# A two-layer vision tower: in its last stage small softmax steps go to GpSimd, the head products are cut into half tiles, and the hand-written order is replaced

## The chip, the cores and the metric

The kernel runs on one core of one Trainium2 chip. Its engines work side by side, each through its own queue in program order: TensorE multiplies matrices (PE in the profile; its weight loads are PEld), VectorE (DVE) and ScalarE (ACT) work element by element, GpSimd (POOL) does the same and also starts some transfers, and SyncE (SP) starts the other transfers (DMA). An instruction that needs another engine's result waits for a semaphore, and all that stands behind it in its queue waits with it. The metric is device time in microseconds (us) for one execution. Three executions of the kernel before took 1803.8, 1806.92 and 1807.66 us; the median is 1806.92 us.

## The reference, cut to what matters

32 images of 256x256 pixels become 256 tokens of 256 numbers each. Layer 0 (attention and a feed-forward part) and the attention of layer 1 come first and are not touched. The change lies in the feed-forward part of layer 1, which has four heads of 64 numbers and, inside every head, four experts:

```python
sx = jnp.einsum('bsh,ndh->bnsd', x, hl_w) + hl_b[None, :, None, :]       # head products
q = jnp.einsum('bnsd,neod->bneso', sx, wq)                               # one query per expert
k = jnp.einsum('bnsd,nod->bnso', sx, wk); v = jnp.einsum('bnsd,nod->bnso', sx, wv)
scores = jnp.einsum('bnesd,bntd->bnest', q, k) * d ** 0.5 + causal
att = jax.nn.softmax(scores, axis=-1)
qkv = jnp.einsum('bnest,bntd->bnesd', att, v)
gs = jax.nn.softmax(gate logits of the four experts, axis=-1)            # first gate
mixed = jnp.einsum('bnsed,bnse->bnsd', out, gs)
hn = layernorm(mixed + resid, ln_g, ln_b)                                # a norm over 64
hx = relu(fx @ fc1_w.T + fc1_b); hx = hx @ fc2_w.T + fc2_b               # zero masks left out here
fout = layernorm(hx + fx, fnorm_g, fnorm_b)
fg = jax.nn.softmax(fout @ fgate_w.T, axis=-1)                           # second gate
return fout * fg                                                         # per head; h is added to it
```

All of it is in 32-bit floats.

## The kernel before, in words

The kernel keeps all 32 images (`H[b]`, 128 tokens by 2 by 256) on the chip and goes through five stages. The last one, called the E stage here, starts at about 1240 us and takes 570 us of the 1812 us. Each image goes through the same 96 or so *pieces*, short functions that issue a few instructions each, listed in `PIECES`. What matters here, in the order in which one image needs it:

- `features_in` (SP loads the image's features), `heads` (PE: four 128x128 products over 256 columns; each 32-bit product shows as two matmul records), `heads_out` (ACT copies them out, SP makes a copy with the halves exchanged), `residual` (for the first four images alone).
- `experts`, `head_values`, `scores` 0 to 4, `exponentials` 0 to 4 (ACT), `outputs` 0 to 3 (PE), `outputs_out` 0 to 7 (ACT). The products of scores, experts and head values are cut into 64x64 tiles, those of `outputs` into 64x64 tiles at first and then 128x64 tiles.
- `gate_logits` and `gate_softmax` 0 to 6: the first gate, on tiles of 128 tokens by 8 (token half and head) by 4 experts. Step 0 takes the maximum, 1 subtracts, 2 is ACT's exponential, 3 the sum, 4 the reciprocal, 5 and 6 multiply. All but step 2 are on VectorE.
- `mixed` 0 and 1 (two VectorE products of 128x1024), `summed` 0 to 2, `squares`, `squares_sum`, `root`, `scaled`: the weighted sum of the experts and its norm.
- `turn_e` (VectorE transposes in blocks, SP writes to memory), `moved_e` (SP reads it back), `turned_e` (ACT), `features_moved` (SP), `first_layer` (PE), `first_layer_out` (ACT, then four SP transfers), `second_layer` (PE, 128x64 tiles), `second_layer_out` (VectorE).
- `head_gate` 0 to 8: the second gate, on tiles of 128 by 2 by 4, and for step 0 and 1 by 4 more. Step 0 multiplies, 1 sums, 2 adds a row, 3 maximum, 4 subtracts, 5 is ACT's exponential, 6 sums, 7 reciprocal, 8 multiplies.
- `last_norm` 0 to 5: three VectorE steps of 128x512, eight of 128x64 that multiply with the gate and add `h`, and the transfer to the output.

No scheduler orders this: `tc.manual_schedule` puts the instructions on each engine in exactly the order in which the pieces are called. The order is a list written out by hand. `ROUND` is one turn of a software pipeline: an entry (-7, 3) means that in round r piece 3 is issued for image r+7. Before the change `heads` is at -7 and the last pieces are at -1, so an image is in work for seven rounds. When `heads` of the last image (31) has been issued, `order_e` leaves the round and issues `END`, a list of all that is left, where an entry (2, 40) means piece 40 of image 31-2. The rounds run for 1240 to 1735 us and `END` from there.

Results of PE go to eight banks that are handed out in turn by `bank()`; a round takes 29 of them, so PE waits if a bank's last contents have not been read. Several tiles have one or two buffers (`fxT`, `both`, `fout`: one; `sx`, `g`, `exT`, `eo`, `ey`: two). For the last image `turn_e` and what follows avoid the way through memory.

The lines that the text names, by their numbers in the kernel before: 118 all products, 1173 and 1179 `heads_out`, 1206 `experts_out`, 1250 `exponentials`, 1285 `outputs_out`, 1349 and 1354 `gate_logits`, 1362 to 1376 `gate_softmax`, 1380 `mixed`, 1388 to 1394 `summed`, 1428 and 1433 `turn_e`, 1440 `moved_e`, 1449 `turned_e`, 1487 and 1490 `first_layer_out`, 1502 `second_layer_out`, 1510 to 1532 `head_gate`, 1537 to 1549 `last_norm`. Lines 151, 152, 842, 856 and 857 are from the stage before (the attention of layer 1), where GpSimd is in use.

Of the kernel before, what the change touches and what calls it, by code (L numbers as in the profile page):

```python
# [33 lines left out]
F32 = mybir.dt.float32  # L34
AF = mybir.ActivationFunctionType
ALU = mybir.AluOpType
AX = mybir.AxisListType
# [3 lines left out]
P = 128  # L41
B, N, D = 32, 256, 256
NC = N // P
HALF = B // 2
KSEL = 127
NH, NE, HD = 4, 4, 64
# [34 lines left out]
def vit_tower(tc, a, out):  # L81

    nc = tc.nc
# [33 lines left out]
    def mm(o, lhsT, rhs, first=True, last=True):  # L117
        nc.tensor.matmul(o, lhsT, rhs, start=first, stop=last)  # L118

    def over(ap, shape, axis):  # L120
        return ap.unsqueeze(axis).to_broadcast(shape)
# [184 lines left out]
    with (  # L306
# [7 lines left out]
        for k, n in enumerate(PARTS):  # L314
            f = sum(PARTS[:k])
            x, w = pw.tile([P, n, N], F32, name=f"patch0_{k}"), pw.tile([P, n, D], F32, name=f"tokW{k}")
# [797 lines left out]
    with (  # L1114
# [49 lines left out]
        def heads(b, im):  # L1164
            p = im.ph = bank()
            for hp in range(2):
                for k in range(2):
                    mm(p[:, hp * N : (hp + 1) * N], hl[:, k, hp * P : (hp + 1) * P], im.f[:, k], k == 0, k == 1)

        def heads_out(b, im):  # L1170
            im.sx = p2.tile([P, 2, N], F32, name="sx")
# [166 lines left out]
        def gate_logits(b, im, i):  # L1338
# [14 lines left out]
            if i == 2:  # L1353
                nc.vector.tensor_reduce(
                    gate_in[b % 2][:, :, 1:], im.lg.rearrange("p g e x -> p g x e"), AX.X, ALU.add
                )

        def gate_softmax(b, im, i):
            x = gate_in[b % 2]
            if i == 0:  # L1360
                im.m = small("sm_m", [P, NG])
                nc.vector.tensor_reduce(im.m, x, AX.X, ALU.max)
            if i == 1:
                im.gate = small("gate", [P, NG, NE])
                nc.vector.tensor_tensor(im.gate, x, over(im.m, [P, NG, NE], 2), ALU.subtract)
            if i == 2:
                nc.scalar.activation(im.gate, im.gate, AF.Exp)
            if i == 3:
                im.m = small("sm_m", [P, NG])
                nc.vector.tensor_reduce(im.m, im.gate, AX.X, ALU.add)  # L1370
            if i == 4:
                nc.vector.reciprocal(im.m, im.m)
            if i == 5:
                nc.vector.tensor_tensor(im.gate, im.gate, im.rden, ALU.mult)
            if i == 6:
                nc.vector.tensor_tensor(im.gate, im.gate, over(im.m, [P, NG, NE], 2), ALU.mult)

        def mixed(b, im, k):
            x = experts_of(im, k, MIX, HD)
# [127 lines left out]
        def head_gate(b, im, i):  # L1507
            if i == 0:
                im.lg = small("lg2", [P, NC, NH, NH])
                nc.vector.tensor_tensor(  # L1510
                    im.lg.rearrange("p c n x -> p (c n) x"), im.whole["ey"][:, :, HD:],
                    over(im.rs, [P, NG, NH], 2), ALU.mult,
                )
            if i == 1:
                im.gate = small("fgate", [P, NC, NH])
                nc.vector.tensor_reduce(im.gate, im.lg.rearrange("p c n x -> p c x n"), AX.X, ALU.add)
            if i == 2:
                nc.vector.tensor_tensor(im.gate, im.gate, over(fg_row, [P, NC, NH], 1), ALU.add)
            if i == 3:
                im.m = small("sm_f", [P, NC])  # L1520
                nc.vector.tensor_reduce(im.m, im.gate, AX.X, ALU.max)
            if i == 4:
                nc.vector.tensor_tensor(im.gate, im.gate, over(im.m, [P, NC, NH], 2), ALU.subtract)
            if i == 5:
                nc.scalar.activation(im.gate, im.gate, AF.Exp)
            if i == 6:
                im.m = small("sm_f", [P, NC])
                nc.vector.tensor_reduce(im.m, im.gate, AX.X, ALU.add)
            if i == 7:
                nc.vector.reciprocal(im.m, im.m)  # L1530
            if i == 8:
                nc.vector.tensor_tensor(im.gate, im.gate, over(im.m, [P, NC, NH], 2), ALU.mult)

        def last_norm(b, im, i):
            f = whole(im, "eblk" if b == B - 1 else "fout", G8)
# [37 lines left out]
            (features_moved,), (count_bad, 0), (count_bad, 1), (count_bad, 2), (count_bad, 3),  # L1573
        )
        ROUND = (
            (-2, 2), (-3, 54), (-1, 72), (-3, 56), (-4, 42), (-6, 4), (-1, 73), (-4, 33), (-1, 74), (-4, 34),
            (-4, 44), (-3, 57), (-4, 45), (-1, 75), (-3, 58), (-3, 59), (-6, 1), (-6, 5), (-4, 43), (-1, 76),
            (-4, 46), (-6, 6), (-5, 16), (-5, 12), (-5, 22), (-1, 77), (-6, 30), (-5, 18), (-2, 67), (-6, 9),
            (-1, 87), (-5, 13), (-4, 47), (-5, 14), (-2, 92), (-2, 69), (-6, 10), (-1, 78), (-5, 19),
            (-6, 11), (-1, 79), (-3, 60), (-4, 48), (-5, 20), (-3, 61), (-6, 7), (-5, 15), (-2, 68),  # L1580
            (-1, 80), (-2, 70), (-1, 89), (-3, 62), (-1, 81), (-4, 49), (-1, 82), (-6, 8), (-1, 88),
            (-3, 63), (-3, 64), (-1, 83), (-5, 31), (-1, 84), (-4, 50), (-5, 32), (-1, 85), (-1, 86),
            (-7, 3), (-8, 0), (-1, 90), (-3, 65), (-5, 21), (-4, 51), (-1, 91), (-5, 41), (-3, 66), (-5, 40),
            (-5, 39), (-4, 52), (-4, 53), (-4, 55), (-2, 71), (-1, 93), (-1, 94), (-1, 95), (-1, 96),
        )
        END = (
            (0, 2), (3, 51), (4, 65), (2, 40), (3, 52), (2, 39), (2, 42), (2, 41), (2, 21), (0, 1), (3, 53),
            (4, 66), (3, 54), (3, 55), (5, 71), (3, 56), (6, 90), (3, 57), (5, 72), (4, 2), (2, 33), (2, 34),
            (0, 4), (5, 73), (5, 74), (3, 58), (2, 43), (5, 75), (2, 44), (3, 59), (1, 15), (5, 76), (2, 46),
            (2, 45), (5, 77), (2, 47), (5, 78), (6, 91), (2, 48), (0, 7), (1, 21), (4, 67), (3, 60), (0, 9),  # L1590
            (2, 49), (3, 61), (4, 92), (2, 50), (5, 79), (4, 69), (0, 10), (0, 5), (0, 8), (2, 51), (3, 62),
            (2, 52), (5, 80), (0, 11), (5, 87), (2, 53), (3, 63), (1, 13), (4, 70), (3, 64), (2, 54),
            (5, 81), (2, 55), (4, 68), (1, 14), (5, 82), (2, 56), (3, 65), (0, 6), (5, 89), (3, 66), (2, 57),
            (1, 19), (1, 16), (1, 12), (1, 20), (0, 12), (5, 83), (5, 88), (4, 71), (1, 18), (1, 22),
            (2, 58), (0, 18), (4, 72), (3, 2), (4, 73), (2, 59), (4, 74), (4, 75), (1, 31), (1, 32), (1, 33),
            (1, 41), (1, 34), (1, 42), (1, 39), (1, 40), (4, 76), (3, 67), (2, 60), (5, 84), (0, 30),
            (5, 85), (3, 69), (2, 61), (5, 86), (5, 90), (1, 44), (3, 68), (0, 13), (1, 43), (2, 62),
            (1, 45), (2, 63), (3, 92), (1, 46), (5, 91), (3, 70), (0, 14), (1, 47), (4, 77), (0, 16),
            (2, 64), (1, 48), (4, 78), (1, 49), (4, 79), (1, 50), (4, 80), (1, 51), (2, 65), (1, 52),
            (1, 53), (4, 81), (2, 66), (0, 22), (0, 15), (4, 82), (0, 19), (1, 55), (1, 54), (0, 20),  # L1600
            (4, 87), (3, 71), (4, 83), (1, 56), (0, 31), (4, 89), (1, 57), (4, 84), (3, 72), (0, 21),
            (1, 58), (0, 32), (0, 40), (3, 73), (4, 85), (1, 59), (4, 88), (1, 60), (0, 41), (0, 42),
            (3, 74), (2, 2), (3, 75), (0, 39), (2, 67), (1, 61), (0, 33), (0, 43), (4, 86), (4, 90), (0, 34),
            (0, 44), (3, 76), (3, 77), (1, 62), (1, 63), (2, 69), (2, 92), (3, 78), (4, 91), (2, 68),
            (2, 70), (1, 64), (1, 65), (3, 79), (0, 46), (0, 45), (0, 47), (3, 80), (1, 66), (0, 48),
            (3, 81), (0, 49), (3, 87), (3, 82), (1, 2), (2, 71), (0, 50), (3, 83), (0, 51), (3, 89), (0, 52),
            (3, 84), (3, 88), (0, 53), (3, 85), (0, 55), (0, 54), (2, 72), (2, 73), (0, 56), (2, 74),
            (3, 86), (0, 57), (2, 75), (3, 90), (2, 76), (0, 58), (3, 91), (1, 67), (2, 77), (0, 59),
            (2, 78), (0, 60), (2, 87), (2, 79), (1, 92), (0, 61), (2, 80), (2, 89), (1, 69), (2, 81),
            (1, 70), (0, 62), (1, 68), (2, 82), (1, 71), (2, 83), (0, 63), (0, 64), (2, 84), (2, 88),  # L1610
            (2, 85), (0, 65), (0, 66), (2, 90), (1, 73), (0, 67), (1, 72), (2, 86), (0, 69), (0, 92),
            (1, 74), (1, 75), (2, 91), (0, 70), (0, 68), (0, 71), (0, 93), (0, 72), (0, 73), (0, 74),
            (0, 94), (1, 76), (0, 75), (1, 77), (0, 76), (0, 95), (1, 78), (0, 77), (0, 87), (0, 78),
            (1, 79), (1, 87), (1, 80), (0, 79), (0, 96), (1, 81), (0, 80), (1, 82), (1, 89), (1, 83),
            (0, 81), (0, 89), (0, 82), (0, 83), (1, 84), (1, 88), (0, 84), (1, 85), (0, 88), (0, 85),
            (1, 86), (1, 90), (1, 91), (0, 90), (0, 86), (0, 91),
        )
        LAST = PIECES.index((heads,))

# [407 lines left out]
```

## Time and profile before

| what | us |
|---|---|
| median of three runs | 1806.92 |
| the profiled execution's own time | 1813.98 |
| its span, from the first to the last instruction | 1812.2 |
| PE, DVE, ACT, POOL busy in the span | 1763.8, 1309.8, 776.5, 445.5 |
| first `heads` product of the E stage | 1241.0 |
| steady rounds, 1300 to 1700 us: 24 images | 400 |
| PE busy in them | 395.68 |
| DVE busy in them | 378.09 |
| ACT busy in them | 336.08 |
| POOL busy in them | 0.00 |
| `heads` of the last image | 1735 |
| 1735 to 1812.2: DVE busy, PE busy | 69.93, 44.95 |

The profiled execution took 0.4% longer than the median. A busy PE does not mean that PE is at its peak, since matmuls overlap and their ends are modelled; what the rows of PE give best is when each group of products starts. The same holds for VectorE in small: an instruction's duration has a tail that the next one overlaps, so that a row of instructions takes less than the sum of their durations. The chain that ended last is an account of what released what; a wait that is no part of it cost nothing.

### The profile page before, as it was taken

Reading aid. Unit: us, or ns where it says so; the run is one execution under the profiler, and the core shown is the slowest. Engines: PE = TensorE matmul, PEld = TensorE weight load, DVE = VectorE, ACT = ScalarE, POOL = GpSimd, SP = SyncE. Lnnn points to the kernel's source line nnn. Section 1 sums busy time; section 2 is a strip of 40 time slices with the busy share of each in tenths; the row PEclk is TensorE's granted clock in tenths of the full one; section 3 lists DMA queues with packets and bytes.
Section 4 is the critical chain, followed back from the end, with each engine's and each line's share of the span. In section 5 each row is a group of like instructions: output and inputs, shape, how many; then the busy total and the mean of one; then the engine's idle time right before and its main releaser. Section 6 shows DMA issues by size and latency. Waiting matters only on the chain.

```text
span 1812.2 us, 43832 instructions
## 1 busy us (share of the span) xinstructions
PE 1763.8 (97%) x18072; PEld 1267.4 (70%) x18072; DVE 1309.8 (72%) x3580; ACT 776.5 (43%) x1607; POOL 445.5 (25%) x506
## 2 busy tenths in 40 slices
PE   9999999999999999999999999999999999999993
PEld 7888566667576676767654555557888888888882
DVE  2335367787878665444458877875699999999998
ACT  0000322222222212121244554555888888888883
POOL 1223234343434335333344433341000000000000
PEclk9999999999999999999999999999999999999995
DMA  8552112121211115233312222112244444444432
GB/s 274 180 154 65 35 30 67 51 72 38 59 47 49 57 50 182 91 119 99 112 57 82 75 88 78 74 71 83 68 114 112 115 111 120 109 118 114 122 99 69
DMA packets 197999, 167.93 MB, mean 93 GB/s; under 512 B 71713, under 2 KB 174881, under 8 KB 197409
## 3 DMA queue, kind: packets, MB, share of 16 engines
q1 hardware_dynamic: 191072, 147.49, 28.4%
q0 software_dynamic: 6144, 16.79, 3.1%
q8 instruction: 144, 2.36, 0.6%
q10 hardware_dynamic: 576, 0.79, 0.2%
q14 instruction: 63, 0.51, 0.1%
HBM read 82.95 MB, written 57.41 MB: 77 GB/s over the span
## 4 chain that ended last, share of the span: by engine, by line
PE 85%; DVE 6%; DMA 4%; ACT 4%; issue 1%; SPq 0%; ACTq 0%; DVEq 0%
PE bank L118 85%; DMA er_turned<-eblk 1%; ACT et L1250 1%; DMA fraw<-er_turned 1%; DMA both<-hx 1%; DVE fout L1545 1%; ACT fxT L1449 0%; DMA patch<-in_patches_dram 0%; PE bank L518 0%; DVE eo L1380 0%; ACT g L1206 0%; DVE eblk L1428 0%; DVE ranges L1403 0%; DVE six L126 0%; ACT eo L1285 0%
## 5 line engine op out<-in xcount | busy, mean ns | idle before, releaser
L118 PE MATMUL bank<-ev,et 64*64 64x72 f32 (+3 forms) x6144 | 186.8, 226 | 0.2
L118 PEld LDWEIGHTS bank<-ev,et 64*64 64x64 f32 (+1 forms) x6144 | 171.6, 135 | 10.9 <-ACT hx L1487 1.2
L118 PE MATMUL bank<-tokW,patch 128*128 128x256 f32 x768 | 170.1, 385 | 2.9 <-DMA patch<-in_patches_dram 2.9
L118 PE MATMUL bank<-g,sw 64*64 64x128 f32 (+2 forms) x1280 | 168.0, 377 | 0.0
L1250 ACT ACTIVATE et<-bank 128x512 f32<-128x512 f32 x320 | 167.4, 624 | 1.2 <-PE bank L118 1.2
L118 PE MATMUL bank<-g,sx 64*64 64x128 f32 (+2 forms) x1280 | 167.6, 377 | 0.0
L118 PEld LDWEIGHTS bank<-tokW,patch 128*128 128x128 f32 x768 | 148.5, 194 | 24.9 <-issue 3.8
L118 PE MATMUL bank<-bxT,w_wuv 128*128 128x512 f32 x300 | 131.4, 592 | 0.0
L869 ACT ACTIVATE hT<-bank,cols 128x512 f32<-128x512 f32 x64 | 43.7, 687 | 187.2 <-PE bank L118 122.3
L118 PE MATMUL bank<-wvo,dm 128*128 128x512 f32 x256 | 114.3, 599 | 0.0
L118 PE MATMUL bank<-w_wo,gT 128*128 128x256 f32 x512 | 113.2, 379 | 0.0
L118 PE MATMUL bank<-attn,bv 128*128 128x256 f32 x512 | 113.1, 379 | 0.0
L118 PE MATMUL bank<-w_w,hT 128*128 128x256 f32 x512 | 112.3, 379 | 0.0
L118 PE MATMUL bank<-xsel,w_w 128*128 128x512 f32 x256 | 111.4, 592 | 0.0
L118 PEld LDWEIGHTS bank<-attn,bv 128*128 128x128 f32 x512 | 97.2, 190 | 19.6 <-issue 7.2
L126 DVE BATCH_NORM_STATS2 six<-h 128x6 f32<-128x256 f32 x256 | 105.7, 413 | 4.4
L118 PEld LDWEIGHTS bank<-w_w,hT 128*128 128x128 f32 x512 | 97.0, 190 | 15.6 <-issue 2.9
L118 PEld LDWEIGHTS bank<-w_wo,gT 128*128 128x128 f32 x512 | 97.2, 190 | 13.4 <-DVE gT L491 0.2
L118 PE MATMUL bank<-w_wuv,bxT 128*128 128x512 f32 x240 | 105.4, 592 | 0.0
L1285 ACT COPY eo<-bank 128x280 f32<-128x280 f32 x256 | 89.3, 396 | 36.4 <-PE bank L118 36.4
L118 PEld LDWEIGHTS bank<-bxT,w_wuv 128*128 128x128 f32 x300 | 57.0, 190 | 64.9 <-issue 64.1
L118 PEld LDWEIGHTS bank<-g,sx 64*64 64x64 f32 x1280 | 92.6, 133 | 10.1
(288 smaller groups left out, 3572.3 us busy)
## 6 DMA issues: line engine op xcount, KB each, us to landing
patch<-in_patches_dram SPq DMA_DIRECT2D x31, 768.0 KB
exT<-normed SPq DMA_DIRECT2D x32, 256.0 KB
sw<-sx SPq DMA_DIRECT2D x64, 128.0 KB
er_turned<-eblk SPq DMA_DIRECT2D x31, 256.0 KB
fraw<-er_turned SPq DMA_DIRECT2D x62, 128.0 KB
both<-fxT SPq DMA_DIRECT2D x62, 128.0 KB
both<-hx SPq DMA_DIRECT2D x124, 64.0 KB
out_dram<-fout SPq DMA_DIRECT2D x31, 256.0 KB
```

The costliest lines, as they stand in the source:

```text
L118: nc.tensor.matmul(o, lhsT, rhs, start=first, stop=last)
L126: nc.vector.bn_stats(six, x)
L869: nc.scalar.activation(s.hT[:, m, :], p, AF.Gelu_apprx_tanh, bias=col("b1", m))
L1250: nc.scalar.activation(t2[:, r, :], p, AF.Exp)
L1285: nc.scalar.copy(im.o[:, g * OC : (g + 1) * OC], p[:, 0:OC])
L1545: nc.vector.scalar_tensor_tensor(f[:, g, :], f[:, g, :], im.gate[:, i - 3, n : n + 1], H[b][:, i - 3, d], ALU.mult, ALU.add)
```

## The change

Three edits, all in the E stage.

1. Eight steps of the two gates move from VectorE to GpSimd for all images but the last: `gate_softmax` 3, 5, 6 and `head_gate` 0, 1, 2, 6, 8. The three that are sums become two GpSimd additions each (`added`: four numbers to two, two to one). So GpSimd gets eleven instructions per image.
2. `heads` computes each 128x128 product as two products of 128x64.
3. `ROUND` and `END` are new lists. In the new round `heads` is at -8 and the last pieces are at -1, so an image is in work for eight rounds. On PE the new round is: `head_values`, `scores` 1, `experts` 1, `first_layer`, `scores` 3, `outputs` 0, `heads`, `outputs` 1, `outputs` 2, `second_layer`, `outputs` 3, `scores` 4, `experts` 0, `scores` 2, `scores` 0. Before it was: `outputs` 2, `outputs` 3, `experts` 0, `scores` 4, `scores` 0, `head_values`, `scores` 1, `scores` 2, `first_layer`, `experts` 1, `scores` 3, `outputs` 0, `outputs` 1, `heads`, `second_layer`.

```diff
@@ heads
                 for k in range(2):
-                    mm(p[:, hp * N : (hp + 1) * N], hl[:, k, hp * P : (hp + 1) * P], im.f[:, k], k == 0, k == 1)
+                    for q in halves:
+                        w = hl[:, k, hp * P + q.start : hp * P + q.stop]
+                        mm(p[q, hp * N : (hp + 1) * N], w, im.f[:, k], k == 0, k == 1)
@@ new, ahead of gate_softmax
+        def on_pool(b):
+            return nc.vector if b == B - 1 else nc.gpsimd
+
+        def added(b, o, x, name):
+            shape = [P, o.shape[1], 2] + list(x.shape[3:])
+            if b == B - 1:
+                nc.vector.tensor_reduce(o, x.rearrange("p c n x -> p c x n") if x.ndim > 3 else x, AX.X, ALU.add)
+                return
+            t = p1.tile(shape, F32, name=name)
+            nc.gpsimd.tensor_tensor(t, x[:, :, 0:2], x[:, :, 2:4], ALU.add)
+            nc.gpsimd.tensor_tensor(o, t[:, :, 0], t[:, :, 1], ALU.add)
@@ gate_softmax
             if i == 3:
                 im.m = small("sm_m", [P, NG])
-                nc.vector.tensor_reduce(im.m, im.gate, AX.X, ALU.add)
+                added(b, im.m, im.gate, "sm_4")
...
-                nc.vector.tensor_tensor(im.gate, im.gate, im.rden, ALU.mult)
+                on_pool(b).tensor_tensor(im.gate, im.gate, im.rden, ALU.mult)
             if i == 6:
-                nc.vector.tensor_tensor(im.gate, im.gate, over(im.m, [P, NG, NE], 2), ALU.mult)
+                on_pool(b).tensor_tensor(im.gate, im.gate, over(im.m, [P, NG, NE], 2), ALU.mult)
@@ head_gate (steps 0, 1, 2, 6 and 8 in the same way)
-                nc.vector.tensor_tensor(im.gate, im.gate, over(fg_row, [P, NC, NH], 1), ALU.add)
+                on_pool(b).tensor_tensor(im.gate, im.gate, over(fg_row, [P, NC, NH], 1), ALU.add)
...
@@ ROUND: all 85 entries replaced (the new ones)
+            (-2, 68), (-5, 47), (-2, 75), (-6, 18), (-7, 9), (-5, 48), (-4, 59), (-1, 78), (-3, 67),
+            (-6, 13), (-5, 49), (-4, 60), (-7, 10), (-6, 19), (-1, 79), (-7, 7), (-3, 92), (-3, 69),
+            (-7, 11), (-7, 8), (-4, 61), (-6, 15), (-5, 50), (-4, 62), (-1, 80), (-1, 87), (-6, 31),
+            (-1, 81), (-1, 89), (-4, 63), (-1, 82), (-3, 70), (-5, 51), (-1, 83), (-4, 64), (-1, 88),
+            (-6, 21), (-8, 3), (-6, 32), (-5, 52), (-6, 39), (-6, 33), (-6, 40), (-4, 65), (-1, 84),
+            (-4, 66), (-6, 41), (-9, 0), (-3, 71), (-6, 42), (-5, 53), (-1, 85), (-1, 90), (-5, 55),
+            (-5, 54), (-1, 86), (-5, 56), (-1, 91), (-6, 34), (-5, 57), (-8, 4), (-6, 43), (-7, 16),
+            (-2, 76), (-4, 2), (-6, 44), (-8, 30), (-3, 72), (-3, 73), (-6, 45), (-6, 46), (-5, 58),
+            (-3, 74), (-8, 1), (-8, 5), (-7, 14), (-7, 22), (-8, 6), (-7, 20), (-2, 77), (-7, 12), (-1, 93),
+            (-1, 94), (-1, 95), (-1, 96),
@@ END: 305 entries before, 324 now
...
```

## The prediction

> **What bounds the kernel now.** I read the page first (busy shares over 40 slices), then the E stage in windows, then PE's and VectorE's waits there, then single groups.
>
> ```profile
> PE   9999999999999999999999999999999999999993
> DVE  2335367787878665444458877875699999999998
> POOL 1223234343434335333344433341000000000000
> ...
> 1500.00:1550.00 50.00, 49.97 (x1280) 42.97 (x1271) 47.66 (x145) 42.92 (x109) 0.00 (x0) 1.00 0.45 117
> sum 400.00, PE 395.68 PEld 337.41 DVE 378.09 ACT 336.08 POOL 0.00; mean PE 49.46 PEld 42.18 DVE 47.26 ACT 42.01 POOL 0.00
> ...
> 1740.00:1790.00 50.00, 34.45 (x832) 28.02 (x823) 49.00 (x154) 31.82 (x83) 0.00 (x0) 0.84 0.39 102
> 1735.00:1812.20 77.20, 44.95 (x1007) 35.08 (x1005) 69.93 (x229) 39.45 (x102) 0.00 (x0) 0.75 0.31 85
> ```
>
> The window columns are length, then busy us (and instructions) of PE, weight loads, DVE, ACT, POOL, then clock, DMA share, GB/s. Steady rounds (the sum over 1300 to 1700, 24 images) take 16.67 us each; PE works 16.49 of them, VectorE 15.75, GpSimd nothing. So PE sets the round and VectorE is 0.9 us behind it. In `END` it is turned round: from 1740 to 1790 VectorE is busy 49 of 50 us and PE 34.
>
> ```profile
> DVE ey L1502 <- PE bank L118: 8.2, 23, 1.0
> DVE ranges L1403 <- ACT esq L1399: 5.6, 7, 1.3
> PEld bank L118 <- ACT fxT L1449: 5.2, 6, 1.3
> PE bank L118 <- ACT fxT L1449: 3.8, 5, 1.0
> ...
> 1402.38 0.23 PE L118 MATMUL bank<-ev,et 128*64 128x72 f32 x1
> 1402.53 1.99 PE L118 MATMUL bank<-exT,w_hl_t 128*128 128x256 f32 x8
> 1404.46 1.17 PE L118 MATMUL bank<-W,both 128*64 128x68 f32 x32
> 1405.56 2.81 PE L118 MATMUL bank<-ev,et 64*64 64x72 f32 x96
> ...
> L118 PE MATMUL bank<-exT,w_hl_t x256: 379/379/483, 1241.0 to 1735.2; 128*128 128x256 f32 x128
> ```
>
> The waits (us in all, times, longest, over the 24 rounds) say that VectorE waits for PE, and PE only for `fxT`, the features that come back through memory. The three timeline groups around `heads` are 128x64, 128x128, 128x64.
>
> **Head products in half tiles.** Removed: 8 records of 128x128 per image. Added: 16 of 128x64. The `W,both` group has the added form: 32 records of 68 columns start within 1.10 us, that is in pairs 0.059 us apart, and 68 columns of the 256 that take 0.216 us are 0.057. So two halves run at once, and 16 half records take 8 x 0.216 = 1.73 us, as the 8 whole ones do. What goes is the change of shape on both sides. In the starts of single records: the first head product starts 0.094 us late, the second 0.320 after it instead of 0.216 (the 483 ns beside 379 in the last line), the first `W,both` 0.093 late, its second pair 0.050 late: 0.34 us per image. In the new round `heads` stands between `outputs` 0, which ends in 128x64, and `outputs` 1, which is 128x64, and `second_layer` between `outputs` 2 and 3, 128x64 too; the four changes between 64x64 and 128x64 per round stay. PE is the bound, so 32 x 0.34 = **-10.9 us**. Bounds: 0 (the cost moves to another boundary) and -10.9; I take -10.9, since no 128x128 product is left in the round.
>
> **The order of the round.** PE's stall chain is `turn_e`, transfer, `moved_e`, transfer, `turned_e`, `first_layer`:
>
> ```profile
> 1420.12 0.65 DVE eblk L1428
> 1420.79 5.02 DMA er_turned<-eblk
> 1426.50 3.62 DMA fraw<-er_turned
> 1430.22 0.82 ACT fxT L1449
> 1431.09 2.64 PE bank L118 x44
> ```
>
> That is 10.97 us. Adding the pieces' rows in the lists' order gives the room for it: before, `turn_e` stands at 15.7 us of VectorE's round (stretched to 16.67) and `first_layer` at 8.5 of PE's next, 9.5 us; now at 8.5 and 2.5 of rounds of 16.2, 10.2 us, and VectorE can be up to 1.5 us ahead of PE, as `second_layer_out` comes later in its list. On SP `moved_e` now stands behind the output transfer and `sw` (issued by about 11 of the round, the first transfer lands at 13 to 14), so neither holds it. PE's idle time in the 24 rounds is 4.3 us; I take half of it away, 0.09 x 29 = **-2.6 us**. Bounds: -5.2, and +9 if `second_layer` (its four transfers are issued 2.4 us long and `first_layer_out` stands behind a VectorE-fed step on ACT) or `fxT` costs 0.3 per round.
>
> **The gates on GpSimd.** Removed from VectorE per image: 145 (L1370), 192, 182, 184, 200, 157, 151 and 167 ns, 1.38 us by duration; by starts less, for four 128x64 `fout` steps of 279 ns take 0.78 us in the chain, 0.70 of their sum. I take 1.0: VectorE falls from 15.75 to 14.75. Added to GpSimd: eleven instructions on 2 to 32 numbers per partition. Nearest rows:
>
> ```profile
> L151 POOL TENSOR_SCALAR rs_d<-st_d 128x4 f32<-128x4 f32 x16 | 3.1, 195 | 113.7 <-DVE st_d L127 112.9 <-issue 0.4
> L152 POOL TENSOR_TENSOR rs_d<-rs_d,minus_half 128x4 f32<-128x4 f32 x16 | 16.6, 1036 | 1.3
> L856 POOL TENSOR_TENSOR h<-h,dx 128x512 f32<-128x512 f32 x28 | 36.3, 1297 | 0.0
> ...
> 1196.61 0.77 DVE L842 TENSOR_SCALAR dx<-h,rs_d,d_one 128x256 f32<-128x256 f32 x2
> 1197.68 2.78 DVE L842 TENSOR_SCALAR dx<-h,rs_d,d_one 128x256 f32<-128x256 f32 x2
> ```
>
> L152 is a power, the additions and products are like L856: (1.297 - 0.195) / 508 = 2.2 ns per number on 0.2 us, so 0.2 to 0.26 each, 2.5 us per image (bounds 2.1 and 11): GpSimd is idle enough even at 11.
>
> What it costs VectorE is the open term. The last two lines are the same instruction twice: 0.77 us beside the 1.0 us power of 1196.70, 2.78 beside the additions L856 and L857, which it had to sit out. So a GpSimd instruction on 512 numbers stops VectorE for its whole length, one on 4 numbers not at all. VectorE works 62% of its E time on instructions with two inputs in SBUF. Bounds: 0, and 2.5 x 0.62 = 1.5 us per image. I take 0.5, near the row with few numbers. The Trainium skill ("SBUF — State Buffer", section "Who interferes with whom") speaks against the change: a VectorE instruction with two SBUF inputs and a GpSimd one that reads SBUF take a shared port as an exclusive lock, and the later one is blocked for the whole instruction. The L856 line agrees, the power beside 0.77 us does not; by the rule alone the term would be the 1.5, by the row 0.
>
> New waits: on GpSimd `head_gate` 8 stands behind `gate_softmax` 3, which waits for ACT's `gate_softmax` 2, behind `exponentials` 3 and `root`, which waits for VectorE's `squares_sum` (done at 7.1 of its round). 7.1 + 0.45 + 0.95 + 0.35 + 0.45 + 0.2 + 0.2 = 9.7; `last_norm` 3, whose turn on VectorE is at 9.2, waits 0.5 us. All behind it on VectorE (`mixed`, `second_layer_out`) moves too. VectorE: 14.75 + 0.5 + 0.5 = 15.75, under the new 16.24 of PE. In the rounds the GpSimd edit is worth nothing.
>
> **`END`.** PE's rows over its entries give 34.7 us before, 35.7 now, so it starts 1.0 us sooner (**-1.0**). VectorE's rows (0.60 per 128x512 step, 1.13 per `mixed`, and so on) give 69.7 before (69.93 busy in the window) and, with the moved steps taken out, 70.9: one more round is in flight. **+1.2**. It has 55 GpSimd instructions: at 0.05 us of blocking each **+2.7** (bounds 0 and 7.5), and for answers that come later than VectorE's own **+1.5** (0 to 5). Nothing covers these: VectorE has 1 us idle in 50.
>
> Sum: -10.9 - 2.6 - 1.0 + 1.2 + 2.7 + 1.5 = **-9.1 us**. The profiled execution took 1813.98 us, 0.4% over the median; it would take 1804.9, and the median 1806.92 would be 1798.
>
> **Rivals.**
> - *VectorE becomes the bound* (slower). Place: two-input steps behind GpSimd's. Price at full blocking: 14.75 + 1.5 + 0.7 = 16.95 us per round, +0.28 x 26 = +7, and +10 in `END`: 1824; at half of it about 1811. For: L856, 62%. Against: the 0.77 line. It decides when blocking and new waits pass 1.5 us per image, 16.24 - 14.75; by then `END` has eaten the rest.
> - *`END` gives it back.* The rounds gain 13.5, but blocking and late answers in `END` cost 11 and not 4: 1805, inside 0.2%, which is 3.6 us and about what a measurement can tell from no change. For: VectorE 49 of 50 busy.
> - *The halves don't run at once*: 16 x 0.216, +1.7 us per image, +55: 1858. Against: `W,both`.
> - *More than forecast*: no blocking (-4), all stalls gone (-3): 1791.
>
> **How the numbers follow.** Forecast (1794 to 1803) 0.47, more than forecast 0.14, `END` gives it back 0.14, VectorE bound 0.23, halves one by one 0.02. Faster 0.61, same 0.14, slower 0.25. The likeliest gives 1798, alone 1791 to 1803. For 8 in 10 I go from 1788 (no blocking and a better-packed `END`) to 1816 (half the VectorE rival and more).
>
> **What would show it.** Head records 128*64 without a long first one, 1.73 us from group to group; rounds of 16.2 to 16.3 us with PE 99% busy; fewer waits for `fxT`; GpSimd at 2.5 us per image; `fout` or `eo` steps mostly at 279 and 1216 ns; from `heads` of image 31 to the end 79 to 82 us. Wrong it would be if two-input VectorE steps grow by GpSimd's whole durations, if VectorE waits for POOL over 1 us per image, or if PE waits for `both` or `fxT` in each round.

## The result, and the profile after

The changed kernel took 1803.68 us (median of 15 runs, 1801.22 to 1807.4), beside 1806.92 us (1803.8 to 1809.64) for the kernel before. The ratio is 0.9984, with a 95% interval of 0.9977 to 0.9991: 3 us less where 9 us were forecast, and inside the 0.2% that the forecast counted as "same". The time lies in the stated range of 1788 to 1816 us and the direction is right, but the gain is a third of what was forecast.

The profiled executions make it look larger: 1801.22 us after, 1813.98 us before. That is the fastest of 15 executions beside one slower than all 15 of before. So both kernels were profiled once more in the experiments (1806.12 and 1803.71 us), and differences below are taken between profiles that lie near their medians.

The first view is the same as before: the busy shares in 40 slices of the kernel after.

```profile
PE   9999999999999999999999999999999999999992
...
DVE  3335376887878565443448878875689998999998
...
POOL 1223133443424335242334433331012221222221
```

GpSimd now has work to the end, and VectorE's slices in the rounds are no fuller than before. Next the windows (length, then busy us and instructions of PE, weight loads, DVE, ACT, POOL, then clock, DMA share, GB/s), first in the rounds from 1300 to 1700 us, then in `END`, which runs from 1717.1 us:

```profile
1500.00:1550.00 50.00, 49.82 (x1331) 41.01 (x1326) 45.29 (x120) 43.14 (x110) 10.09 (x33) 1.00 0.41 114
...
sum 400.00, PE 398.37 PEld 331.83 DVE 359.87 ACT 342.37 POOL 78.93; mean PE 49.80 PEld 41.48 DVE 44.98 ACT 42.80 POOL 9.87
...
1720.00:1770.00 50.00, 36.23 (x929) 29.13 (x928) 49.43 (x131) 32.81 (x85) 11.18 (x35) 0.87 0.38 108
1717.10:1799.40 82.30, 45.00 (x1060) 35.42 (x1054) 74.76 (x221) 42.24 (x111) 17.21 (x55) 0.79 0.30 86
```

PE is busy for 99.6% of the rounds, so PE sets them, as forecast. `END` is VectorE's, as before, and takes 82.3 us. The waits of the rounds, the three groups of products around `heads`, and `heads` by its records:

```profile
DVE ranges L1417 <- ACT esq L1413: 19.7, 22, 2.2
...
DVE fout L1559 <- POOL fgate L1546: 8.7, 23, 0.4
...
PEld bank L118 <- ACT g L1208: 5.0, 24, 0.3
...
1408.22 2.22 PE L118 MATMUL bank<-ev,et 64*64 64x72 f32 x64
1410.27 1.90 PE L118 MATMUL bank<-exT,w_hl_t 128*64 128x256 f32 x16
1412.00 2.91 PE L118 MATMUL bank<-ev,et 128*64 128x72 f32 x96
...
L118 PE MATMUL bank<-exT,w_hl_t x512: 379/379/430, 1236.3 to 1718.6; 128*64 128x256 f32 x171
```

`heads` takes 1.73 us from start to start (1410.27 to 1412.00), as forecast, against 1.92 before. PE's waits for `fxT` are down to 0.2 us. In their place stands a wait that was not there: for `g`, the copy of `experts_out`, once in each round, by 0.2 us on the mean.

The forecast said that PE waited only for `fxT` before the change. The same view of the kernel before has one more line, a wait of PE's weight loads in 22 of the 24 rounds, between `heads` and `second_layer`:

```profile
PEld bank L118 <- ACT eo L1285: 7.3, 22, 0.3
```

It goes with the whole head products. With half products in the old order the line is gone; with whole products in the new order the weight loads are idle for 0.33 us behind `heads` again, and there the profile names no other engine as the cause.

The table is the working view of all that follows. It comes from when the first `heads` record of each image starts: the first one, the five intervals in which the pipeline fills, the 26 rounds after them, the round that no wait disturbs (the lowest value that recurs), and the time from the last image's `heads` to the end. "Over" is what the 26 rounds took beyond 26 undisturbed ones. Us, from one profile each; the ratio is of the times, to before.

| kernel | ratio (95%) | first | fill | 26 rounds | undisturbed | over | `END` |
|---|---|---|---|---|---|---|---|
| before, first profile | 1 | 1241.0 | 62.2 | 430.5 | 16.26 | 7.6 | 78.6 |
| before, again | 1 | 1235.8 | 62.2 | 428.1 | 16.26 | 5.2 | 78.3 |
| after, first profile | 0.9984 (0.9977 to 0.9991) | 1236.3 | 60.9 | 419.9 | 16.10 | 1.2 | 82.3 |
| after, again | | 1237.4 | 61.0 | 420.9 | 16.11 | 2.1 | 82.7 |
| before + half tiles | 1.0000 (0.9991 to 1.0009) | 1237.4 | 61.8 | 430.3 | 15.91 | 16.6 | 79.5 |
| before + GpSimd | 0.9996 (0.9988 to 1.0005) | 1236.9 | 62.2 | 427.3 | 16.25 | 4.8 | 79.4 |
| before + both of these | 0.9992 (0.9981 to 1.0003) | 1238.9 | 61.5 | 426.8 | 15.90 | 13.4 | 77.7 |
| new order alone | 1.0070 (1.0057 to 1.0083) | 1235.6 | 62.1 | 429.3 | 16.46 | 1.5 | 87.8 |
| new order + GpSimd | 1.0031 (1.0019 to 1.0044) | 1235.9 | 62.1 | 430.1 | 16.46 | 2.2 | 82.4 |
| new order + half tiles | 1.0006 (0.9997 to 1.0015) | 1235.7 | 61.0 | 421.4 | 16.11 | 2.6 | 89.1 |

From "before, again" to the two profiles of after: the rounds give 7.2 to 8.2 us, the fill 1.2 to 1.3, and `END` takes 4.0 to 4.4 back. The first profile of before had 5.2 us more ahead of the E stage, in code that the change does not touch, and 2.4 us more of stalls.

### The profile page after: what moved, and what is told of

Read it like the earlier page. It is cut to its first block, busy times and chain, and to the rows that moved or that the text cites. A ratio compares the mean times of both kernels' runs of the same rounds, so it can differ in the third digit from the quotient of the medians.

```text
span 1799.4 us, 44514 instructions
## 1 busy us (share of the span) xinstructions
PE 1751.3 (97%) x18328; PEld 1245.9 (69%) x18328; DVE 1273.6 (71%) x3332; ACT 774.3 (43%) x1607; POOL 547.8 (30%) x847
## 4 chain that ended last, share of the span: by engine, by line
PE 87%; ACT 5%; DVE 5%; issue 1%; DMA 1%; SPq 0%; ACTq 0%; POOL 0%; DVEq 0%
PE bank L118 87%; ACT et L1252 2%; ACT g L1208 1%; ACT fxT L1463 1%; DVE fout L1559 1%; PE bank L518 0%; DVE eo L1394 0%; DVE ranges L1417 0%; DMA patch<-in_patches_dram 0%; DVE six L126 0%; ACT dex L950 0%; DVE fout L1553 0%; DMA both<-hx 0%; DVE dz L996 0%; DVE two L1402 0%
## 5 line engine op out<-in xcount | busy, mean ns | idle before, releaser
L118 PE MATMUL bank<-ev,et 64*64 64x72 f32 (+3 forms) x6144 | 197.5, 226 | 2.6 <-ACT et L1252 0.7
L118 PEld LDWEIGHTS bank<-ev,et 64*64 64x64 f32 (+1 forms) x6144 | 179.7, 135 | 19.2 <-ACT g L1208 5.7
L118 PE MATMUL bank<-g,sw 64*64 64x128 f32 (+2 forms) x1280 | 176.4, 380 | 0.0
L118 PE MATMUL bank<-g,sx 64*64 64x128 f32 (+2 forms) x1280 | 175.4, 379 | 0.0
L1252 ACT ACTIVATE et<-bank 128x512 f32<-128x512 f32 x320 | 172.6, 627 | 4.1 <-PE bank L118 2.6
L118 PEld LDWEIGHTS bank<-w_wo,gT 128*128 128x128 f32 x512 | 97.2, 190 | 13.4 <-DVE gT L491 0.2
```

The source lines that it names most:

```text
L1252: nc.scalar.activation(t2[:, r, :], p, AF.Exp)
```

## The experiments

The theory at the start: half tiles give 0.35 us per round, but in the new order a wait of PE for ACT's copies takes half of it; the rival: the 0.35 us is not to be had, or is lost somewhere else.

### Half tiles alone, in the kernel before

```diff
-                    mm(p[:, hp * N : (hp + 1) * N], hl[:, k, hp * P : (hp + 1) * P], im.f[:, k], k == 0, k == 1)
+                    for q in halves:
+                        w = hl[:, k, hp * P + q.start : hp * P + q.stop]
+                        mm(p[q, hp * N : (hp + 1) * N], w, im.f[:, k], k == 0, k == 1)
```

> The kernel before, with the head products in half tiles and nothing else. Theory A (the half tiles are worth what the starts of single records say, 0.34 us per image, and PE is the bound): the group `heads` takes 1.73 us from start to start and the group after it 0.95 (before 1.92 and 1.10), undisturbed rounds 15.92 us instead of 16.26, the time falls by about 10.5 us (0.58%), to 1796 to 1797. Theory B (in after, a wait of PE for ACT's second copy of `experts_out` 1 eats half of it, and that wait comes from the steps being closer together, not from the new order): here too about 0.16 us per round is left, the time falls by about 5 us, to 1802. Rival C (another wait takes the whole place): within 2 us of before.

Measured: 1806.54 us beside 1806.5, ratio 1.0000. It is rival C: another wait takes the whole place. The undisturbed round is 15.91 us, within 0.01 us of what the forecast's terms give (16.26 - 0.34), yet only seven of the 26 rounds are undisturbed. The waits from 1300 to 1700 us:

```profile
ACT fxT L1451 <- DMA fraw<-er_turned: 12.0, 10, 2.1
PEld bank L118 <- ACT fxT L1451: 10.9, 10, 2.0
...
PE bank L118 <- ACT fxT L1451: 8.8, 9, 1.8
...
PEld bank L118 <- DMA both<-hx: 2.3, 5, 0.5
```

PE waited 5.2 us for `fxT` (its weight loads' line) in the kernel before, 3.2 in its second profile, now 10.9. The features' way through memory does not get shorter when PE's round does.

### Whole head products, in the kernel after

The edit is the one above, undone.

> The changed kernel, with the head products in whole tiles again. Theory A (the 0.28 us wait of PE for `experts_out` 1 in each round is a fixed cost of the new order): rounds grow by the whole 0.34 us, to 16.44 us, and the time by 10 to 11 us over after, to about 1814. Theory B (the wait is ACT not getting its copies out in time, and takes up whatever PE gains ahead of it): rounds grow by 0.1 to 0.2 us only, the wait shrinks to under 0.1 us, and the time grows by 2 to 5 us, to 1806 to 1809.

Measured: 1812.35 us, ratio to before 1.0031, 8.5 us (0.47%) more than after. The undisturbed round is 16.46 us, 0.35 more than after's. Theory A: in the new order the half tiles are worth what was forecast, 26 x 0.35 = 9.1 us in the rounds and 1.1 in the fill, and the wait for `g` is a cost of the order that does not shrink when PE has more time ahead of it (that wait's line still has 4.2 us). The group that waits is the 64x64 part of `outputs` 0: 1.03 us from start to start with whole and with half products in the new order, 0.85 in the old one; the other groups, some longer and some shorter by a change of shape, sum to the same. So the new order makes the round 0.19 us longer by itself (0.19 with half products, 0.20 with whole ones).

### One copy of `experts_out` on VectorE

```diff
             for h, p in enumerate(im.pg[hp]):
-                nc.scalar.copy(im.g[:, 2 * hp + h, :, :].rearrange("p j n -> p (j n)"), p)
+                o = im.g[:, 2 * hp + h, :, :].rearrange("p j n -> p (j n)")
+                if hp == 1 and h == 1 and 0 < b < B - 3:
+                    nc.vector.tensor_copy(o, p)
+                else:
+                    nc.scalar.copy(o, p)
```

> The changed kernel, with one of the two copies of `experts_out` 1 (the one that ends the chain of ACT copies for which PE waits in `outputs` 0) on VectorE instead of ACT, in the rounds. If that chain of copies is what keeps the rounds of after at 16.10 instead of 15.85: PE's wait of 0.28 us there goes, rounds of 15.85 to 15.95 us, 4 to 6.5 us less than after, 1797 to 1800. Rival (VectorE, 14.5 us busy per round, slips by the 0.7 us copy and its waits, so that answers come later): rounds stay at 16.1 or grow, 1803 to 1810.

Measured: 1796.8 us (1796.31 to 1800.31), ratio to before 0.9951 (0.9937 to 0.9965), 9 us less than before and 6 less than after (0.33%). ACT's queue ahead of `outputs` 0, first in after, then with the copy moved:

```profile
1405.75 0.87 ACT L1463 ACTIVATE fxT<-fraw,cols 128x512 f32<-128x512 f32 x1
1406.46 1.14 ACT L1252 ACTIVATE et<-bank 128x512 f32<-128x512 f32 x2
1407.41 1.16 ACT L1208 COPY g<-bank 128x512 f32<-128x512 f32 x2
```

```profile
1402.87 1.14 ACT L1256 ACTIVATE et<-bank 128x512 f32<-128x512 f32 x2
1403.83 0.66 ACT L1212 COPY g<-bank 128x512 f32<-128x512 f32 x1
...
1403.54 0.69 DVE L1210 COPY g<-bank 128x512 f32<-128x512 f32 x1 [0.42 <-PE bank L118]
...
1404.63 1.83 PE L118 MATMUL bank<-ev,et 64*64 64x72 f32 x63
```

In after, `outputs` 0 starts at 1408.22 us and needs four banks. `experts` 1, `first_layer` and `scores` 3, which stand just ahead of it, hold two each, so that two of the eight are left; its other two are those of `experts` 1, which ACT has read only at 1408.57, behind `fxT` and two exponentials. PE starts six of the group's records by 1408.34 and the next at 1408.62; `outputs` 0 does not read `g`, so it is the bank that it waits for:

```profile
1408.62 0.89 PEld L118 LDWEIGHTS bank<-ev,et 64*64 64x64 f32 x32 [0.21 <-ACT g L1208]
```

With one copy on VectorE both are read before PE comes (the later one ends at about 1404.5, PE starts at 1404.63), the group takes 0.64 us instead of 1.03, and the round 15.88 instead of 16.10; 0.17 us of the gain goes again in the two groups behind it. (The old order's 0.85 us holds a wait too, for a bank of `first_layer`: with half tiles alone ACT's step on it ends at 1530.95 us and PE goes on at 1531.00.) VectorE had the room: 375.9 us busy of 400. The 26 rounds take 416.6 us, 3.3 to 4.3 less than in after, as 3.7 us are lost in disturbed rounds here; the rest of the 6 us lies in the fill and ahead of the E stage, where profiles differ by more than that.

### The kernel before, profiled again

> The kernel before, unchanged, for a second profile. If the 7.7 us of PE's stalls on `fxT` in the 26 rounds and the 4.8 us of the opening stage are the kernel's own: a span of about 1812 us again with rounds of 17.2 to 17.7 us among them. If they were that one execution's: a span near 1805, and the rounds nearer to 16.26 us.

Measured: 1806.12 us, span 1804.3. Neither expectation fits whole. The opening stage's 5 us were that one execution's. The stalls are mostly the kernel's own: 5.2 us over in the 26 rounds instead of 7.6, 17.9 us in the longest round.

### The old order with both other edits

> The kernel before with the half tiles and with the gates on GpSimd, in its old order: the changed kernel without the new order. With the half tiles alone the undisturbed round came to 15.91 us, as short as forecast, but PE's waits for `fxT` and `both` took the gain back. Theory A (VectorE, 15.7 us busy in a round of 15.91, was the cause: it has no slack to send the features off in time): with about 1 us less on VectorE the waits go back to 2 us or less over the 26 rounds, rounds of 15.95 to 16.05 us on the mean, and `END` changes by -1 to +3: 8 to 13 us less than before, 1793 to 1798. Theory B (the old order's places of `turn_e` and `first_layer` are too near each other, whatever VectorE has to do): waits as with the half tiles alone, 1803 to 1808.

Measured: 1807.18 us beside 1808.96, ratio 0.9992. Theory B, nearly: relief for VectorE takes 3 us off the waits and no more. From the start of `turn_e` to `first_layer` the undisturbed schedule leaves 9.78 us in the kernel before, 9.5 here, and 11.82 in after; where PE waited for `fxT` in the old order (before, half tiles, and this kernel, from 1300 to 1700 us), the way through memory, from the start of `turn_e` to the end of `turned_e`, had taken 9.6 to 11.5 us. So the old order has not enough room in it, and what PE gains makes the room shorter by about as much: 9.43 us with half tiles alone.

### The kernel after with the gates on VectorE

```diff
-            return nc.vector if b == B - 1 else nc.gpsimd
+            return nc.vector
@@ added
-            if b == B - 1:
+            if b <= B - 1:
```

> The changed kernel with both gates' sums and products back on VectorE; its order and half tiles are kept. The forecast had the GpSimd edit at nothing in the rounds (VectorE at 15.75 under PE's 16.24) and at +4.2 us in `END` (blocking and late answers). Theory A (so it is): rounds as in after, 16.10 us, `END` 3 to 5 us shorter, 1799 to 1801. Theory B (VectorE at 15.7 us of work can't hold a round of 16.1 without slips, as with the half tiles alone): rounds of 16.4 us or more on the mean, 7 us or more over after, 1809 to 1815, with VectorE over 95% busy in the rounds.

Measured: 1809.51 us, ratio to before 1.0006 (0.9997 to 1.0015), 0.22% more than after. In the rounds it is theory A: 421.4 us, after 419.9 and 420.9. In `END` it is neither: 89.1 us instead of 82.3 to 82.7. `END` in four kernels, each from the last `heads` to the end (before again; new order alone; new order and half tiles; and, further above, after), in three fences in this order:

```profile
1726.00:1804.30 78.30, 46.62 (x1016) 36.26 (x1012) 71.43 (x233) 40.87 (x106) 0.00 (x0) 0.75 0.32 85
```

```profile
1726.99:1814.90 87.91, 47.81 (x1048) 37.55 (x1044) 79.20 (x261) 42.39 (x111) 0.00 (x0) 0.76 0.30 80
```

```profile
1718.00:1807.00 89.00, 47.58 (x1058) 36.40 (x1052) 79.25 (x261) 42.23 (x111) 0.00 (x0) 0.75 0.30 79
```

VectorE is busy 91, 90, 89 and (after) 91% of `END`. The new order leaves it 79.2 us of work there instead of 71.4, since one more image is in flight; the GpSimd edit takes 4.5 of these 7.8 us away, and `END` gets 5.4 us (whole products) to 6.8 us (half tiles) shorter.

### The kernel before with the gates on GpSimd

> The kernel before with the gates on GpSimd alone; old order, whole head products. PE sets the round (16.26 us undisturbed, that can't change). Theory A (VectorE's slack is what PE's stalls on `fxT` hang on): the 5 to 7.6 us of stalls in the 26 rounds fall to under 2; 3 to 5 us less than before in the rounds, `END` -1 to +3: 1802 to 1806. Theory B (the stalls hang on the places in the lists): stalls as before; blocking on VectorE and late answers show alone: 1806 to 1811.

Measured: 1808.55 us beside 1808.96, ratio 0.9996. Theory B in the rounds (4.8 us over instead of 5.2), and nothing that can be measured is lost by blocking either.

### The kernel after, profiled again

> The changed kernel, unchanged, for a second profile: its first profile was the fastest of its 15 runs. If the differences between runs lie in the opening stage and in single rounds: again an undisturbed round of 16.10 us and an `END` of 82.3 us, and 1 to 4 us more in the opening or in slipped rounds.

Measured: 1803.71 us, beside a median of 1803.68, with an undisturbed round of 16.11 and an `END` of 82.7 us, as expected; 1.1 us more ahead of the E stage and 1.0 more in slipped rounds.

### The new order alone

The two edits above together: whole products, and the gates on VectorE.

> The new order alone: whole head products, gates on VectorE. The forecast took the order of the round as a gain of 2.6 us (half of PE's stalls) and the order of `END` as +0.2 us (PE 1.0 us earlier, VectorE's rows 1.2 us longer). Theory A (the order by itself is a loss, which the other two edits pay for): undisturbed rounds of 16.45 us as in the run with whole products, 4 to 5 us longer over 26 rounds, of which fewer stalls give 3 to 5 back; `END` 88 to 89 us instead of 78.5, since VectorE has one image more in flight and nobody takes work from it; 9 to 12 us more than before. Theory B (the forecast's terms): 2 to 3 us less than before.

Measured: 1817.79 us beside 1805.25, ratio 1.0070 (1.0057 to 1.0083). Theory A, nearly in each of its parts: undisturbed rounds of 16.46 us, 1.5 us of stalls instead of 5.2, an `END` of 87.8 us.

### `first_layer` one place later in the old order

The kernel with the old order, half tiles and GpSimd, and two lines of `ROUND`:

```diff
-            (-1, 87), (-5, 13), (-4, 47), (-5, 14), (-2, 92), (-2, 69), (-6, 10), (-1, 78), (-5, 19),
-            (-6, 11), (-1, 79), (-3, 60), (-4, 48), (-5, 20), (-3, 61), (-6, 7), (-5, 15), (-2, 68),
+            (-1, 87), (-5, 13), (-4, 47), (-5, 14), (-2, 92), (-6, 10), (-1, 78), (-5, 19),
+            (-6, 11), (-1, 79), (-3, 60), (-4, 48), (-5, 20), (-3, 61), (-6, 7), (-2, 69), (-5, 15), (-2, 68),
```

> The old order with half tiles and the gates on GpSimd, and `first_layer` one place later in PE's list, behind `experts` 1 (0.86 us). From the start of `turn_e` to `first_layer` the old order leaves 9.5 us, the new one 11.8, and the way of the features through memory takes 9.4 to 11.5 us in the rounds where PE waited. Theory A (this room is what the new order is worth): PE's waits for `fxT` fall from 11 us to under 4 over the 24 rounds of 1300 to 1700. What is late next: `both` has 0.86 us less up to `second_layer` (3.5 instead of 4.4 us for four transfers), so PE waits there, 0.3 to 0.8 us in each round, and the rounds come out at 16.2 to 16.6 us all the same. Rival: the waits for `fxT` stay (the transfers are late because SP's queue or VectorE is), no change of them by more than a third.

Measured: 1799.28 us (1797.99 to 1802.6) beside 1805.25, ratio 0.9973 (0.9960 to 0.9987). PE's waits from 1300 to 1700 us, ahead without and behind with the move:

```profile
PEld bank L118 <- ACT fxT L1463: 6.5, 8, 1.4
PE bank L118 <- ACT fxT L1463: 4.8, 7, 1.2
PEld bank L118 <- DMA both<-hx: 3.2, 7, 0.7
```

```profile
PEld bank L118 <- DMA both<-hx: 2.3, 6, 0.7
...
PE bank L118 <- DMA both<-hx: 1.2, 3, 0.6
...
PEld bank L118 <- ACT fxT L1463: 0.3, 1, 0.3
```

The main part of theory A holds: with 10.36 us of room instead of 9.5 the waits for `fxT` fall from 6.5 to 0.3 us, and the rounds from 426.8 to 420.2 us. What I expected next did not come. `both` has as much time as before, because ACT issues `hx` 0.70 us behind the start of `first_layer` and not 1.51: it stood in ACT's queue waiting its turn anyway. The old `END` stays and takes 77.5 us. So half tiles, GpSimd and one entry moved do about as much as the change does with two new lists, and by the medians more (-0.27% and -0.16%; the intervals overlap).

This run also shows which banks are used again. Here too `experts` 1, `first_layer` and `scores` 3 stand just ahead of `outputs` 0, but PE goes on with its fourth bank at 1328.28 us, when ACT's step on `first_layer` has ended (1328.22) and its copies of `experts` 1 have not begun (1328.70 to 1329.79), and the group takes 0.84 us as in the old order. So the banks do not simply go round in turn, as I had put it ahead of the forecast. What fits the runs is that a group gets the banks whose last reader stands first in the lists: here `first_layer_out`, in after `experts_out` 1. This was not tested by itself.

### `second_layer` moved as well

```diff
-            (-2, 2), (-3, 54), (-1, 72), (-3, 56), (-4, 42), (-6, 4), (-1, 73), (-4, 33), (-1, 74), (-4, 34),
-            (-4, 44), (-3, 57), (-4, 45), (-1, 75), (-3, 58), (-3, 59), (-6, 1), (-6, 5), (-4, 43), (-1, 76),
+            (-2, 2), (-3, 54), (-3, 56), (-4, 42), (-6, 4), (-4, 33), (-1, 71), (-4, 34), (-3, 57),
+            (-4, 44), (-1, 72), (-1, 73), (-4, 45), (-1, 74), (-3, 58), (-1, 75), (-3, 59), (-6, 1), (-6, 5), (-4, 43), (-1, 76),
...
-            (-5, 39), (-4, 52), (-4, 53), (-4, 55), (-2, 71), (-1, 93), (-1, 94), (-1, 95), (-1, 96),
+            (-5, 39), (-4, 52), (-4, 53), (-4, 55), (-1, 93), (-1, 94), (-1, 95), (-1, 96),
```

> As the run before, and `second_layer` moved too: between `outputs` 2 and 3, as the new order has it (1.6 us later on PE), with the two `second_layer_out`, `squares` 1 and `squares_sum` 1 behind it and `gate_softmax` 6 and the first `mixed` ahead of them; `END` is that of before. Theory A (the room for `fxT` and `both` is all that the old order lacked): rounds of 15.8 to 15.9 us undisturbed, since the change of shape behind `second_layer` goes too, 15.9 to 16.0 on the mean; `END` 77.5 to 79.5 us; 12 to 16 us less than before, the fastest of all, 1792 to 1796 beside a before of 1807. Rival (the answers of `second_layer` come 1.6 us later to VectorE and to ACT, whose next steps then wait): rounds over 16.2 us, within 4 us of before.

Measured: 1822.35 us, ratio 1.0091 (1.0077 to 1.0105). A miss: rounds of 17.06 us. The group behind `second_layer` loses its change of shape, as expected, but PE now waits for ACT in every round (ahead, the kernel with one entry moved has 27.4 us in the first of these lines, and no line for the gate's exponential):

```profile
ACT eo L1287 <- PE bank L118: 54.3, 47, 1.4
...
PEld bank L118 <- ACT gate L1381: 8.1, 21, 0.4
PEld bank L118 <- ACT hx L1501: 7.9, 46, 0.2
PEld bank L118 <- ACT et L1252: 5.4, 26, 0.3
```

ACT waits 1.2 us more per round (54.3 over 23.4 rounds against 27.4 over 24.8) for the banks of `outputs` 2 and 3, of which the second now comes behind `second_layer`, and the rounds are 1.16 us longer. PE's three lines above are 0.9 us per round. That ACT's wait is the cause fits in size; it was not tested alone.

### Less work for VectorE in `END`

On top of the version with the moved copy, for images 27 to 29:

```diff
@@ last_norm 3 and 4
                 for n in range(NH):
                     ...
+                    if B - 5 <= b < B - 2:
+                        nc.scalar.activation(f[:, g, :], f[:, g, :], AF.Identity, scale=im.gate[:, i - 3, n : n + 1])
+                        continue
@@ last_norm 5
+                if B - 5 <= b < B - 2:
+                    y = f.rearrange("p (c n) d -> p c (n d)", n=NH)
+                    nc.vector.tensor_tensor(y, y, H[b], ALU.add)
                 nc.sync.dma_start(
```

> The changed kernel with one copy of `experts_out` 1 on VectorE (0.9951 of before) and, for the images 27 to 29, the last step of `last_norm` otherwise: ACT multiplies by the gate, in eight 128x64 steps, and VectorE adds `H` in one 128x512 step ahead of the output's transfer, instead of eight VectorE steps of 0.2 us per image. The rounds stay as they are (15.88 us undisturbed, about 16.0 on the mean). Theory A (`END` lasts as long as VectorE has work, 75 of its 83 us): 3 x (1.57 - 0.68) = 2.7 us less work, `END` of 80 to 81 us instead of 82.9, 0.9935 to 0.994 of before. Theory B (the chain of the last images decides, and ACT's 2 us per image lie in it): `END` of 82.5 to 85 us, 0.995 to 0.9965 of before.

Measured: 1805.81 us, ratio to before 0.9987 (0.9978 to 0.9997). The rounds are the same (416.4 us beside 416.6), `END` takes 90.5 us instead of 82.9. Theory A is wrong, and B has the direction but not the size. In `END`:

```profile
1713.60:1804.00 90.40, 45.86 (x1058) 35.55 (x1052) 72.05 (x200) 47.74 (x135) 16.96 (x55) 0.73 0.27 78
...
DVE fout L1555 <- DMA out_dram<-fout: 4.5, 3, 2.3
...
DVE fout L1572 <- ACT fout L1564: 3.4, 1, 3.4
...
DVE ranges L1421 <- ACT esq L1417: 3.0, 1, 3.0
```

VectorE does have 2.8 us less to do (72.05 instead of 74.89), but these three lines alone are 10.9 us, and in the version without the edit only 0.6 of them is there. `fout` has one buffer, so a later end of one image's last step means a later output transfer and a later start of the next one's; that is read from the waits and not tested by itself. "VectorE is busy 90% of the time" did not mean that taking work from it helps wherever it is taken.

## Why the prediction was wrong

**Head products in half tiles, -10.9.** Right, in size too. With the new order they give 0.35 us per round and 1.1 us in the fill, 26 x 0.35 + 1.1 = 10.2 in all (8.5 by the two ratios). The starts of single records were the right view. What the term leaves out is that it needs an order in which PE can go faster: in the old one the same edit is worth 1.0000.

**The order of the round, -2.6.** This is the step that failed. "The four changes between 64x64 and 128x64 per round stay" was true, and by summing PE's rows the two rounds came out alike. But undisturbed the new order's round is 0.19 us longer, 26 x 0.19 = 5.0 us, which the sum does not have. The sum put PE's waits for banks at nothing; my bound of +9 named `second_layer` and `fxT`, and it was neither, but the banks of `experts` 1 behind ACT's queue. The lists held it: six of the eight banks are in use when `outputs` 0 wants four, `experts_out` 1 is the first of their readers, and `turned_e` and two exponentials stand ahead of its copies on ACT. I followed the queues of VectorE, SP and POOL past each moved step, and ACT's only for `first_layer_out` and the exponential of the first gate. The gain was undersized too: stalls fall by 3.1 to 4.0 us over the 26 rounds, not 2.6, since the room grew by 2.0 us and not by 0.7.

**The gates on GpSimd, 0 in the rounds.** Right: 421.4 against 419.9 to 420.9 us in the new order, and in the old one 428.1 against 427.3; only where VectorE was short of time, in the old order with half tiles, it gave 3.5 us. The wait of `last_norm` 3 for `head_gate` 8 is there at 0.38 us each time (8.7 us, 23 times; forecast 0.5). The blocking of 0.5 us per image is not: in the new order VectorE's `eo` steps take 1216 ns with and 1220 without GpSimd's work, the `fout` steps 273 and 274. The two rows from which I priced it could not tell: both are `TENSOR_SCALAR` steps, which read one tensor, and I applied them to steps that read two.

**`END`, -1.0 + 1.2 + 2.7 + 1.5 = +4.4.** Measured +4.0 to +4.4, for wrong reasons. VectorE's work there grew by 3.3 us (71.4 to 74.8) with the moved steps already out, where I had 1.2; without the GpSimd edit it is 7.8 (79.2). The earlier start, -1.0, is in no run by itself: from the first `heads` to the last the new order alone takes 491.4 us, the kernel before 490.3, and the longer round (5.2) and fewer stalls (-3.7) account for that but for 0.4 us. And blocking and late answers, 4.2 us in my sum, are nothing to be seen: VectorE's idle time in `END` went from 6.9 to 7.5 us. So the GpSimd edit, which I had costing 4.2 us there against the rows that it takes away, is what keeps the new `END` from 88 to 89 us.

**The base.** I set the sum against a profiled execution of 1813.98 us and carried it to the median. 2.4 us of the stalls in it were more than a typical execution has.

The sum again, with what was measured: half tiles -10.2, the round's 5.0, stalls -3.6, `END` +4.2 make -4.6 us. The measured -3.2 (-1.6 to -4.2) differs by 1.4 us; ahead of the E stage, in code that no run changed, `heads` starts at 1235.8 us in the second profile of before and at 1236.3 and 1237.4 in those of after.

**The rivals.** "`END` gives it back" has the time (1805), but not the mechanism: `END` cost what I had in the forecast, and the rounds gained less. "VectorE becomes the bound" and "the halves don't run at once" are out: VectorE is busy 359.87 us of 400 in the rounds, and 16 half records take 1.73 us. (The last one's price was mis-added: 1798 + 55 is 1853, not 1858.)

## What to carry to other kernels

Before costing a faster group on the bounding engine, measure how much time the schedule leaves to each transfer that comes back to that engine: if it is already the time that the transfer takes, the gain is lost until one entry of the order is moved. For a new order, follow every queue past the moved steps, ACT's as well, and find for each group whose PSUM banks (the eight that PE writes its results to) it takes over and where their last reader stands in its queue. A price from one profiled execution is worth a second profile of the same kernel: here 5 us of 12.8 lay in code that was the same.

## What the runs showed of the hardware that I had not expected

The blocking that I feared for VectorE falls on GpSimd. In after, the addition that sums the second gate's logits starts while VectorE is in a 128x1024 product; its output is 128x8, and it took as long as the product:

```profile
1335.28 0.22 POOL L1369 TENSOR_TENSOR lg<-lg 128x16 f32<-128x16 f32 x1
1335.58 1.23 POOL L1370 TENSOR_TENSOR fgate<-lg 128x8 f32<-128x8 f32 x1
1336.89 0.20 POOL L1532 TENSOR_TENSOR fgate<-fgate,fg_row 128x8 f32<-128x8 f32 x1
...
1335.54 1.21 DVE L1394 TENSOR_TENSOR eo<-eo,gate 128x1024 f32<-128x1024 f32 x1
```

That is so in 22 of the 24 rounds from 1300 to 1700 us; GpSimd's other steps take 0.19 to 0.30 us on the mean. The product began 0.04 us ahead of it and was not longer for it. With the old order and GpSimd, where that addition meets no such step, it takes 0.20 us (and the product `lg`, which meets the 128x1024 sum `two` there, 0.83 to 0.86 on the mean instead of 0.24). The Trainium skill ("SBUF — State Buffer", section "Who interferes with whom") says that a VectorE instruction with two SBUF inputs contends with a GpSimd instruction that reads SBUF, and that the order of issue decides which of them blocks. The trace agrees: the product was first, and the addition took 1.23 us instead of 0.20. On GpSimd, idle for 80% of the rounds, this costs nothing that the round shows.

The other number is how far the edits depend on each other: they are worth +0.70% (order alone), 0.00% (half tiles alone), -0.04% (GpSimd alone) and -0.16% together; one copy moved to another engine on top of them makes it -0.49%, the fastest version here.
